# Pair stage of a gated scan and Hadamard FFN kernel: outer products put together by accumulating DMAs

## The chip, the cores and the metric

The kernel runs on one core of one Trainium2 chip. The metric is the device time of one execution in microseconds (us); of several runs the median counts. A profiled execution is a single run with the hardware profiler on. Its engines are named PE (TensorE, matmuls), PEld (its weight loads), DVE (VectorE), ACT (ScalarE), POOL (GpSimd) and SP (SyncE, which here only issues DMAs). A DMA can be issued from SP's queue or from POOL's; the instructions of one engine start in the order of its queue.

## The reference

One transformer layer in float32, with batch 4, sequence 512, model width 512 and hidden width 2048. A gated linear scan takes the place of attention, and the feed-forward part has a Walsh-Hadamard transform ahead of its down projection. The first 490 us of the kernel do everything up to the feed-forward part of batches 2 and 3; what follows concerns that part alone.

```python
def _L0_ffn_ref(x, W1, W2, W3):
    up_gate = jnp.einsum('bsd,hd->bsh', x, W1)
    up_lin = jnp.einsum('bsd,hd->bsh', x, W3)
    hidden = jax.nn.silu(up_gate) * up_lin
    hidden = fwht(hidden)
    out = jnp.einsum('bsh,dh->bsd', hidden, W2)
    return out
...
x = x + _layernorm(_L0_attn_ref(_layernorm(x, axis=-1), ...), axis=-1)
x = x + _layernorm(_L0_ffn_ref(_layernorm(x, axis=-1), ...), axis=-1)
```

The transform `fwht` is folded into `W2` once, early in the kernel, so the down projection reads a transformed `W2`.

## The kernel before

**Seven products.** Every matrix product is cut into 2x2 blocks and made of seven block products instead of eight (Strassen-Winograd). Of each left factor four blocks A11, A12, A21, A22 are loaded and four sums S1 to S4 are made (`combine_left`: L158, L159, L162, L163, four instructions on a tile). Of each right factor the blocks are B11 to B22 and the sums T1 to T4 (`combine_right`, L168 to L173). `ORDER` (L33) names the seven products P1, P2, P6, P5, P7, P3, P4 in the order in which they run, with the PSUM bank of each. Bank X is the running sum of P1, P6, P7 and P4; bank Z that of P5 and P3; bank Y holds P2. So P6 can be added into X only when P1's value has been copied out, P7 only after P6's copy, and so on. After each product its bank goes to its quarter (i, j) of the result. "Fresh" products (P1, P6, P5, P4) are the first to write a quarter, the others (P2, P7, P3) are added to it by VectorE.

**The pair stage.** Batches 2 and 3 go through the up projection together: they are the two column blocks of one wide right factor, so there is one more level of seven products around the seven. The stage is the last loop of the program: it calls `load_down_pair(g)` and `ffn_pair(g, ...)` for g = 0 to 3, then runs the parts that are left, then the tail (residual, layer norm and output of batches 2 and 3). Each run g makes two hidden tiles of each of the two batches (`NS = 2`). Its leading loop goes over the seven outer products in the order `OUTER` (P1, P2, P6, P7, P5, P4, P3), called steps 0 to 6; the inner loop goes over the seven inner ones in `ORDER`. One inner product of one outer product is a leaf: two matmul instructions of 128x128 by 128x256, four records in the profile, all at L879. A run has 49 leaves, counted 1 to 49; leaf 43 is the first of outer P3, which comes last. A bank is evicted after every leaf.

**Leaf weights.** `load_leaf_w(n)` (n = 7g + step + 3, so three outer products ahead; n is counted within a run in what follows, so that step 0 of a run asks for n=3) issues four loads `wl` of 128 KB from SP's queue and then `combine_left` on GpSimd: four instructions on the loaded tile. The tiles rotate through five buffers.

**Accumulators.** The seven outer products also add up to four quarters; each quarter is a 1 MB tile in SBUF of 128 x 2048 numbers (both of `w1` and `w3`, two hidden tiles, 512 columns). Before, there are four of them, `q0` to `q3`. Outer P1 goes into q0 and is copied by ScalarE where fresh (L889), otherwise added by VectorE (L892). Outer P2 goes into q1, with q0 as the base that is added to its fresh products. P6 is added into q0. P7 goes into q3, fresh products by ScalarE. P5 goes into q2 with q0 as the base, and beside it GpSimd adds q3 into q0 (L894) and q2 into q3 (L896), quarter by quarter, eight adds per run. P4 is added into q0, P3 into q2. So in five of the seven outer products all seven evictions are VectorE's.

**What the quarters become.** `hidden(k, h, j)` takes a finished quarter: a SiLU on ScalarE over its first half (L852, 128 x 1024) and two multiplications on VectorE (L860), which write half of a hidden tile `ht` each. When both halves are there, `combine_left` runs on the `ht` tile on GpSimd. Each run thus makes four `ht` tiles: two of batch 2 and two of batch 3. `hidden` is called for q1 and q0 after outer P4, for q3 and q2 at the end of a run.

**What runs between the leaves.** The down projection of the run before (`ffn_out(b, g, True)`) is cut into 28 parts for each batch, one matmul instruction each. In `ffn_pair` they stand in `down` and are spread over leaves `start = 3` to 48: 56 of them in runs g1 to g3 (batch 2's 28, then batch 3's 28), and in g0 those of batch 1. The last 56 follow after g3. Parts read the `ht` tiles and their sums (S1, S2, ...), and every fourth part ends with an eviction (L492 on VectorE, L494 on ScalarE). In g0 the output stage of batch 1 lies beside them (`sums`, `acts`): statistics, `inverse_root` (whose power, L263, is on GpSimd), layer norm, residual, and the output DMAs, which GpSimd issues (L724).

**Right factor.** `combine_pair_late()` is called once ahead of g0: eleven subtractions on VectorE, which make the T sums of the outer level and those of the inner level for the later outer products. `reload_x` brings back the inputs of batch 1.

**What sets the order.** PE and SP run in the order in which the program is written (`tc.manual_schedule` for these two engines). The order on VectorE, ScalarE and GpSimd is chosen when the kernel is built, by a scheduler that looks at data dependences, at `tc.high_priority(offset=...)` and at `tc.issue_after(...)`, which holds an instruction behind another. Evictions have the highest offset (`URGENT`).

Of the kernel before, what the change touches and what calls it, by code (L numbers as in the profile page):

```python
# [11 lines left out]
F32 = mybir.dt.float32  # L12
AF = mybir.ActivationFunctionType
ALU = mybir.AluOpType
P = 128
# [13 lines left out]
T3 = B12  # L29
# [15 lines left out]
def kernel(  # L45
# [40 lines left out]
    )  # L86

# [161 lines left out]
    def behind(what):  # L249


        return tc.issue_after(read[what].ins)
# [210 lines left out]
    def seven(name, multiply, quarter, done=None, add=False, by_tile=False, parts=False):  # L463
# [9 lines left out]
        def make(what, a, bb, which, first, only=None):  # L473
# [23 lines left out]
            if what in ("P2", "P7", "P3") and not by_tile:  # L497
                while scaled and scaled[0][0] == 0:
                    acts.append(scaled.popleft()[1])
                for entry in scaled:  # L500
                    entry[0] -= 1
                for _ in range(min(pace[what], len(sums))):
                    with tc.issue_after(read[what].ins):
                        sums.popleft()()
# [169 lines left out]
    def ffn_out(b, part, parts=False):  # L674
# [21 lines left out]
        def done(i, j, tile=None):  # L696
# [3 lines left out]
            def store(residual, t):  # L700
# [11 lines left out]
                if len(held) == NT:  # L712
                    with tc.issue_after(norm[0].last.ins):
                        for make in held:
                            make()
                    stores(range(NT))
# [59 lines left out]
    def raw(r):  # L776
        return xq[r][:, 0:4]
# [13 lines left out]
    def combine_pair_late():  # L791

        blocks[2] = pair_tile("xt", "xq_3")
        xq.update({T2: blocks[2][:, 0], T1: blocks[2][:, 1]})
        nc.vector.tensor_sub(raw(T2), raw(B21), raw(T4))
        nc.vector.tensor_sub(raw(T1), raw(B22), raw(T2))
        inner(blocks[1], (1,))
        inner(blocks[2])
        combine_right(xq[T4], nc.vector)
# [33 lines left out]

    def ffn_pair(g, down):

        total, start = len(down), 3
        given = 0
        q = {}
        first_of = {"P1": (0, None), "P7": (3, None), "P2": (1, 0), "P5": (2, 0)}
        to_of = {"P1": 0, "P2": 1, "P6": 0, "P7": 3, "P5": 2, "P4": 0, "P3": 2}  # L840

        def accumulator(k):
            pool, tag, bufs = (work, "d", 2) if k == 0 else (xpool, "x", 3)
            q[k] = pool.tile([P, 2, 2, T], F32, tag=tag, name=f"q{k}_{g}", bufs=bufs)

        def part(k, i, j):
            return q[k][:, :, i, ts(j, H)]

        def hidden(k, h, j):

            d, b = q[k], PAIR[j]
            nc.scalar.activation(d[:, 0], d[:, 0], AF.Silu)  # L852
            for n in range(NS):
                m = NS * g + n
                if (b, m) not in hts:
                    hts[b, m] = work.tile(
                        [P, 7, H], F32, tag="ht", name=f"ht_{b}_{m}", bufs=4
                    )
                t = hts[b, m]
                nc.vector.tensor_mul(  # L860
                    t[:, h : h + 3 : 2],
                    d[:, 0, n].rearrange("p (t f) -> p t f", t=2),
                    d[:, 1, n].rearrange("p (t f) -> p t f", t=2),
                )
            return [hts[b, NS * g + n] for n in range(NS)]

        for step, (outer, _, right, _, _) in enumerate(OUTER):
            load_leaf_w(7 * g + step + AHEAD)
            w, x = leaf_w.pop(7 * g + step), xq[right]
            to, base = to_of[outer], None  # L870
            if outer in first_of:
                to, base = first_of[outer]
                accumulator(to)
            ps = {}
            for s, (what, a, bb, which, first) in enumerate(ORDER):
# [9 lines left out]
                fresh = what in ("P1", "P6", "P5", "P4")  # L885
                y = part(to, i, j)
                with tc.high_priority(offset=URGENT):
                    if fresh and outer in ("P1", "P7"):
                        read["copy"] = nc.scalar.copy(y, ps[which])  # L889
                    else:  # L890
                        z = part(base, i, j) if fresh and base is not None else y
                        last = nc.vector.tensor_add(y, ps[which], z)  # L892
                if outer == "P5" and fresh:
                    nc.gpsimd.tensor_add(part(0, i, j), part(0, i, j), part(3, i, j))  # L894
                if outer == "P5" and what in ("P2", "P7", "P3", "P4"):
                    nc.gpsimd.tensor_add(part(3, i, j), part(3, i, j), part(2, i, j))  # L896
                if acts and s in (0, 2, 4):
                    with behind("copy"):
                        acts.popleft()()
                if sums and what in ("P2", "P7", "P3"):  # L900
                    with tc.issue_after(last.ins):
                        sums.popleft()()
                leaf = 7 * step + s + 1
# [4 lines left out]
            if outer == "P4":  # L908
                hidden(1, 0, 0)
                for t in hidden(0, 1, 0):  # L910
                    combine_left(t, nc.gpsimd)
        hidden(3, 1, 1)
        for t in hidden(2, 0, 1):
            combine_left(t, nc.gpsimd)
# [166 lines left out]
    with tc.issue_after(load_x(0).ins):  # L1081

        nc.scalar.activation(unused_t, half_t, AF.Silu)
# [201 lines left out]
    with tc.high_priority(offset=SOON):  # L1285
        combine_pair_late()
# [3 lines left out]
    for g in range(NU // NS):  # L1290
        load_down_pair(g)
        ffn_pair(g, deque(down))
# [41 lines left out]
```

## Time and profile before

| | us |
|---|---|
| runs | 792.66, 791.98, 791.95; median 791.98 |
| profiled execution | 792.25, of which the span of the profile is 790.5 |
| granted TensorE clock | 0.996 of full speed on average |
| runs g0 to g3 begin (first matmul of leaf 1) | 490.23, 553.95, 621.94, 689.44 |
| leaf 49 of each begins | 553.08, 621.08, 688.58, 755.25 |
| last 56 parts | 756.1 to 780.5 |
| tail, after the last matmul | 780.5 to 790.5 |

Evictions and combinations of the pair stage, by their rows:

| line, engine, operation | how many | mean of one, us |
|---|---|---|
| L889 ACT copy, a bank to an accumulator | 32 | 0.585 |
| L892 DVE add, a bank and an accumulator | 164 | 0.69 |
| L852 ACT SiLU, half an accumulator | 16 | 1.06 |
| L860 DVE multiplication into `ht` | 32 | 0.71 |
| L894, L896 POOL adds of accumulators | 16 + 16 | 1.27 |
| L158, L159, L162, L163 POOL, on a leaf weight tile | 26 to 28 each | 0.75 to 0.81 |
| the same on an `ht` tile | 16 each | 0.73 to 0.85 |
| L263 POOL power | 6 | 0.87 |

How to read it: the times of the table are counted from the start of the profiled execution. A leaf without a part beside it takes 0.86 from its first matmul to the next leaf's; with the parts a run takes about 67. Rows of a busy engine say nothing of the end unless another engine waits for it, so what matters is which engine TensorE waits for, and where.

### The profile page before, as it was taken

The page shows a single profiled execution, that of the slowest core. Times are in us where ns is not written, and L with a number is a line of the kernel's source. Part 1 is how long each engine was busy: PE and PEld are TensorE (multiplying, and loading weights), DVE is VectorE, ACT ScalarE, POOL GpSimd, SP SyncE. Part 2 cuts the span into 40 slices and gives each one's busy share as a digit, 9 for nine tenths or more (in the row PEclk, how much of TensorE's full clock was granted, in tenths as well). Part 3 has the DMA queues.
Part 4 walks back from the last instruction along what each step waited for, and adds up shares of the span by engine and source line. Part 5 has one row for each costly group of instructions (what it writes and reads, how often), then busy time and mean ns, then how long its engine had stood idle before and what let it go on. Part 6 is the DMA issues. An engine that isn't in the chain of part 4 may idle for free.

```text
span 790.5 us, 10222 instructions
## 1 busy us (share of the span) xinstructions
PE 776.3 (98%) x3608; PEld 670.1 (85%) x3608; DVE 564.2 (71%) x1093; ACT 246.9 (31%) x348; POOL 245.5 (31%) x319
## 2 busy tenths in 40 slices
PE   9999999999999999999999999999999999999994
PEld 7888788888888888888888888888788888888884
DVE  6789889799789774477455459868755655765676
ACT  4374754543436212344223412011321200111112
POOL 2111202112213110001001005088947646672452
PEclk9999999999999999999999999999999999999998
DMA  9997445776997982538246736341521412141012
GB/s 296 398 340 299 156 198 180 218 258 244 339 336 289 340 325 102 160 150 347 94 187 200 267 78 221 131 122 33 195 80 54 157 53 58 49 166 54 1 53 108
DMA packets 78148, 144.93 MB, mean 183 GB/s; under 512 B 6160, under 2 KB 55952, under 8 KB 77712
## 3 DMA queue, kind: packets, MB, share of 16 engines
q1 hardware_dynamic: 68032, 96.82, 38.1%
q0 software_dynamic: 9344, 46.14, 14.9%
q10 hardware_dynamic: 720, 1.31, 0.4%
q8 instruction: 29, 0.48, 0.2%
q14 instruction: 23, 0.19, 0.1%
HBM read 97.06 MB, written 47.19 MB: 182 GB/s over the span
## 4 chain that ended last, share of the span: by engine, by line
PE 88%; DVE 5%; DMA 2%; POOL 1%; issue 1%; SPq 0%; ACT 0%; POOLq 0%; DVEq 0%
PE X_f L517 13%; PE X_po L684 13%; PE X_u L879 11%; PE X_a L517 10%; PE Z_po L684 7%; PE Z_f L517 6%; PE Z_u L879 5%; PE Z_a L517 5%; PE X_y L624 3%; PE Y_f L517 3%; PE Y_po L684 3%; PE Y_a L517 3%; PE Y_u L879 3%; PE Z_y L624 2%; DMA w2p<-in_W_dram 1%
## 5 line engine op out<-in xcount | busy, mean ns | idle before, releaser
L684 PE MATMUL X_po<-w,ht 128*128 128x256 f32 x512 | 132.1, 379 | 0.1
L517 PE MATMUL X_f<-xt_f,w 128*128 128x256 f32 x512 | 121.2, 380 | 0.1
L879 PE MATMUL X_u<-xq,wl 128*128 128x256 f32 x448 | 114.4, 381 | 2.3 <-ACT q L889 0.8
L517 PEld LDWEIGHTS X_f<-xt_f,w 128*128 128x128 f32 x512 | 96.8, 190 | 14.5 <-DVE d_f L492 0.5
L684 PEld LDWEIGHTS X_po<-w,ht 128*128 128x128 f32 x512 | 97.2, 190 | 13.7 <-DVE f L492 0.5
L879 PEld LDWEIGHTS X_u<-xq,wl 128*128 128x128 f32 x448 | 84.2, 190 | 17.1 <-issue 3.6
L892 DVE TENSOR_TENSOR q<-X_u,q 128x512 f32<-128x512 f32 x88 | 60.8, 691 | 42.6 <-PE X_u L879 41.7
L494 ACT COPY d_f<-X_f 128x512 f32<-128x512 f32 x48 | 28.0, 584 | 131.8 <-PE X_f L517 115.7
L684 PE MATMUL Z_po<-w,ht 128*128 128x256 f32 x256 | 66.4, 379 | 0.0
L492 DVE TENSOR_TENSOR f<-X_po,f 128x512 f32<-128x512 f32 x51 | 34.9, 685 | 36.9 <-PE X_po L684 36.9
L517 PE MATMUL Z_f<-xt_f,w 128*128 128x256 f32 x256 | 60.5, 379 | 0.0
L879 PE MATMUL Z_u<-xq,wl 128*128 128x256 f32 x224 | 57.6, 379 | 0.0
L684 PEld LDWEIGHTS Z_po<-w,ht 128*128 128x128 f32 x256 | 48.6, 190 | 6.8 <-DVE f L492 0.2
L517 PEld LDWEIGHTS Z_f<-xt_f,w 128*128 128x128 f32 x256 | 48.6, 190 | 6.6
L263 POOL TENSOR_TENSOR rs_f<-rs_f,power 128x2 f32<-128x2 f32 x16 | 13.4, 840 | 117.8 <-DVE nm_f L364 73.5
L852 ACT ACTIVATE q<-q 128x1024 f32<-128x1024 f32 x16 | 16.9, 1057 | 103.8 <-DVE q L892 58.2
L879 PEld LDWEIGHTS Z_u<-xq,wl 128*128 128x128 f32 x224 | 42.5, 190 | 6.0 <-DVE q L892 0.3
L892 DVE TENSOR_TENSOR q<-Z_u,q 128x512 f32<-128x512 f32 x48 | 33.1, 689 | 20.1 <-PE Z_u L879 19.5
L158 POOL TENSOR_TENSOR wl<-wl 128x256 f32<-128x256 f32 x28 | 21.3, 762 | 77.4 <-DMA wl<-s_w 70.2
L494 ACT COPY d_a<-X_a 128x512 f32<-128x512 f32 x36 | 21.1, 585 | 67.8 <-PE X_a L517 67.6
L889 ACT COPY q<-X_u 128x512 f32<-128x512 f32 x24 | 14.0, 584 | 89.4 <-PE X_u L879 76.8
L179 POOL DMA_DIRECT2D s_w<-w x24 | 13.1, 547 | 72.5 <-DVE w L163 56.9
(205 smaller groups left out, 1459.2 us busy)
## 6 DMA issues: line engine op xcount, KB each, us to landing
w<-s_w SPq DMA_DIRECT2D x32, 896.0 KB, 6.4
s_w<-w POOLq DMA_DIRECT2D x24, 896.0 KB, 6.9
wl<-s_w SPq DMA_DIRECT2D x112, 128.0 KB, 2.7
w<-in_W_dram SPq DMA_DIRECT2D x32, 256.0 KB, 6.4
wi<-s_wi SPq DMA_DIRECT2D x6, 896.0 KB, 9.3
wf<-s_wf SPq DMA_DIRECT2D x6, 896.0 KB, 5.4
wg<-s_wg SPq DMA_DIRECT2D x6, 896.0 KB, 6.3
w_h<-w2p POOLq DMA_DIRECT2D x8, 512.0 KB, 5.7
```

The costliest lines, as they stand in the source:

```text
L158: eng.tensor_add(t[:, S1], t[:, A21], t[:, A22])
L179: nc.gpsimd.dma_start(out=saved[key], in_=t)
L263: read["power"] = nc.gpsimd.tensor_tensor(r, r, power_t[:, 0:n], ALU.pow)
L492: read[what] = nc.vector.tensor_add(to, ps[which], to)
L494: read["copy"] = nc.scalar.copy(to, ps[which])
L517: nc.tensor.matmul(ps[:, n, :], w[:, a, c, :], xt[:, bb, c, :], start=first and n == 0 and c == 0, stop=c == 1, skip_group_check=True,)
L624: nc.tensor.matmul(ps[:, t, :], og[:, a, c, ts(t, P)], w[c][:, bb, :], start=first and t == 0 and c == 0, stop=c == 1, skip_group_check=True,)
L684: nc.tensor.matmul(ps[:, t, :], hts[b, m][:, a, ts(t, P)], w[m][:, W2[bb], :], start=first and k == 0, stop=m == ms[-1], skip_group_check= ...
L852: nc.scalar.activation(d[:, 0], d[:, 0], AF.Silu)
L879: nc.tensor.matmul(ps[which][:, k, :], w[:, k, a, :], x[:, bb, :], start=first and k == 0, stop=True, skip_group_check=True,)
L889: read["copy"] = nc.scalar.copy(y, ps[which])
L892: last = nc.vector.tensor_add(y, ps[which], z)
```

## The change

It concerns `ffn_pair` and what lies beside it in the pair stage.

- Five accumulators A to E instead of four. Each outer product has one of its own (`ROLE`): P1 in A, P2 in B, P6 in C, P7 in D, P5 in E, and then P4 in A and P3 in C again. They are allocated once, and from run to run the roles rotate: A takes what was B, B what was D, D what was A.
- The fresh products of every outer product but P3 are copied by ScalarE; all else is added by VectorE. There is no base any more, and GpSimd's adds are gone.
- The outer products are put together by DMAs that add (`accum_op=ALU.add`) one whole accumulator of 1 MB to another, from SBUF to SBUF, issued by GpSimd (`gather`). They are issued after the last leaf of an outer product: B += A after P2, C += A after P6, D += C after P7, C += E after P5, and E += D and A += D after P4. P3 is added to what C holds then.
- The SiLUs and multiplications are placed by hand after certain leaves (`after_leaf`): B's after leaf 37, 39 and 40 of its run, C's, A's and E's after leaves 2 to 13 of the next run (written 51 to 62, from which 49 is taken). In the last run B's multiplications and all of C, A and E are placed among the last 28 parts and behind them.
- In g1 to g3 the parts begin after leaf 10 instead of leaf 3. In g3 only half of the 56 parts are spread over the leaves; the other 28 run right after leaf 49.
- `combine_pair_late` gives a list of eleven instructions, one after each of leaves 1 to 11 of g0.
- Within `ffn_pair` all engines run in the written order (`tc.manual_schedule()` without a list of engines), and the holds `issue_after` do nothing there (`after`).

```diff
+    acc, after_leaf = {}, {}
+    ROLE = {"P1": "A", "P2": "B", "P6": "C", "P7": "D", "P5": "E", "P4": "A", "P3": "C"}
+    GATHER = {
+        "P2": (("B", "A"),), "P6": (("C", "A"),), "P7": (("D", "C"),),
+        "P5": (("C", "E"),), "P4": (("E", "D"), ("A", "D")),
+    }
+
+    def hidden(d, g, b, h, combine):
+
+        def gate():
+            read["copy"] = nc.scalar.activation(d[:, 0], d[:, 0], AF.Silu)
+
+        def product(n):
...
+            nc.vector.tensor_mul(
+                t[:, h : h + 3 : 2],
+                d[:, 0, n].rearrange("p (t f) -> p t f", t=2),
+                d[:, 1, n].rearrange("p (t f) -> p t f", t=2),
+            )
+            if combine:
+                combine_left(t, nc.gpsimd)
+
+        return [gate] + [partial(product, n) for n in range(NS)]
+
     def ffn_pair(g, down):
 
-        total, start = len(down), 3
+        last = g == NU // NS - 1
+        total, start = len(down), 10 if g else 3
...
+        if not acc:
+            for k in "ABCDE":
+                pool, tag, bufs = (work, "d", 2) if k in "AC" else (xpool, "x", 3)
+                acc[k] = pool.tile([P, 2, 2, T], F32, tag=tag, name=f"acc_{k}", bufs=bufs)
+        else:
+            acc.update({"A": acc["B"], "B": acc["D"], "D": acc["A"]})
+        q = dict(acc)
+
+        def gather(to, part):
+            nc.gpsimd.dma_start(
+                out=q[to].rearrange("p n i t -> p (n i t)"),
+                in_=q[part].rearrange("p n i t -> p (n i t)"),
+                accum_op=ALU.add,
+            )
...
+        place(hidden(q["B"], g, PAIR[0], 0, False), (37, 50, 50) if last else (37, 39, 40))
+        place(hidden(q["C"], g, PAIR[1], 0, False), (51, 53, 54))
+        place(hidden(q["A"], g, PAIR[0], 1, True), (55, 57, 58))
+        place(hidden(q["E"], g, PAIR[1], 1, True), (59, 61, 62))
+        if last:
+            total -= 28
 
         for step, (outer, _, right, _, _) in enumerate(OUTER):
             load_leaf_w(7 * g + step + AHEAD)
...
-                fresh = what in ("P1", "P6", "P5", "P4")
-                y = part(to, i, j)
-                with tc.high_priority(offset=URGENT):
-                    if fresh and outer in ("P1", "P7"):
-                        read["copy"] = nc.scalar.copy(y, ps[which])
-                    else:
-                        z = part(base, i, j) if fresh and base is not None else y
-                        last = nc.vector.tensor_add(y, ps[which], z)
-                if outer == "P5" and fresh:
-                    nc.gpsimd.tensor_add(part(0, i, j), part(0, i, j), part(3, i, j))
-                if outer == "P5" and what in ("P2", "P7", "P3", "P4"):
-                    nc.gpsimd.tensor_add(part(3, i, j), part(3, i, j), part(2, i, j))
+                y = q[ROLE[outer]][:, :, i, ts(j, H)]
+                if what in ("P1", "P6", "P5", "P4") and outer != "P3":
+                    nc.scalar.copy(y, ps[which])
+                else:
+                    nc.vector.tensor_add(y, ps[which], y)
+                leaf = 7 * step + s + 1
+                for make in after_leaf.pop(leaf, ()):
+                    make()
...
-            if outer == "P4":
-                hidden(1, 0, 0)
-                for t in hidden(0, 1, 0):
-                    combine_left(t, nc.gpsimd)
-        hidden(3, 1, 1)
-        for t in hidden(2, 0, 1):
-            combine_left(t, nc.gpsimd)
+            for pair in GATHER.get(outer, ()):
+                gather(*pair)
...
+        if not last:
+            after_leaf.update({k - 49: after_leaf.pop(k) for k in sorted(after_leaf)})
+            return
+        b0, b1, gate_c, *c, gate_a, a0, a1, gate_e, e0, e1 = pending
+        steps = {2: b0, 4: b1, 6: gate_c, 9: gate_a, 12: a0, 14: a1, 18: gate_e}
+        for k in range(len(down)):
+            down.popleft()()
+            if k in steps:
+                steps[k]()
+        for make in (*c, e0, e1):
+            make()
...
+    for leaf, make in enumerate(combine_pair_late()):
+        after_leaf.setdefault(leaf + 1, []).append(make)
...
     for g in range(NU // NS):
         load_down_pair(g)
-        ffn_pair(g, deque(down))
+        with tc.manual_schedule():
+            in_order.append(g)
+            ffn_pair(g, deque(down))
+            in_order.clear()
```

## The prediction

> Times are in us from the start of the profiled execution unless they are durations. A leaf is the two matmuls of one inner product; g0 to g3 are the four runs of `ffn_pair`, with leaves 1 to 49 each; n counts the leaf weight tiles of a run, n=3 being the one asked for at its first step. T0 is the end of a run's leaf 49.
>
> **What bounds the kernel now.** I read the busy times first, then the pair stage cut into its four runs, what TensorE waited for there, the timeline around the largest gap, and the DMA rows.
>
> ```profile
> PE 776.3 (98%) x3608; PEld 670.1 (85%) x3608; DVE 564.2 (71%) x1093; ACT 246.9 (31%) x348; POOL 245.5 (31%) x319
> ```
>
> ```profile
> core 0: us, PE busy (x) PEld busy (x) DVE busy (x) ACT busy (x) POOL busy (x), PEclk, DMA share, GB/s
> 490.00:554.00 64.00, 63.10 (x287) 53.54 (x286) 50.59 (x82) 8.24 (x12) 41.09 (x48) 1.00 0.29 91
> 554.00:622.00 68.00, 67.32 (x310) 58.20 (x309) 42.74 (x69) 15.63 (x24) 47.50 (x60) 1.00 0.30 94
> 622.00:689.40 67.40, 66.61 (x309) 58.36 (x308) 41.02 (x63) 8.80 (x12) 41.95 (x52) 1.00 0.26 83
> 689.40:756.10 66.70, 66.70 (x309) 58.45 (x309) 41.62 (x64) 8.81 (x12) 33.11 (x40) 1.00 0.22 75
> 756.10:780.50 24.40, 24.35 (x113) 21.09 (x111) 20.18 (x46) 3.73 (x5) 9.60 (x14) 1.00 0.24 87
> ```
>
> TensorE is the bound, at full clock, and the change leaves its 3608 matmul records as many as they are. In the chain of waits eight records take 1.73, 0.216 each, so 309 records need 66.7: g3 (689.40 to 756.10) has no gap at all, g2 has 0.7, g1 about 1.1, g0 (64.0 for 286) about 2.2. Counted from start to start of neighbouring matmuls in the timeline, the whole stage loses 5.2. More than that cannot be won; vector and scalar work are off the path except where a gap shows them on it:
>
> ```profile
> PEld X_u L879 <- issue: 3.6, 7, 1.2
> PEld X_u L879 <- DVE q L892: 1.4, 2, 0.9
> ```
>
> ```profile
> 622.94 1.06 ACT L852 ACTIVATE q<-q 128x1024 f32<-128x1024 f32 x1 [1.08 <-DVE q L892]
> 623.45 0.38 PE L879 MATMUL Y_u<-xq,wl 128*128 128x256 f32 x1
> ...
> 623.90 0.57 ACT L889 COPY q<-X_u 128x512 f32<-128x512 f32 x1
> ...
> 624.62 0.45 PE L879 MATMUL X_u<-xq,wl 128*128 128x256 f32 x1 [0.79 <-ACT q L889]
> ```
>
> This is the kind of gap: bank X carries a running sum, so P6 may not be added before P1 has been copied out. Here a SiLU stands ahead of the copy, which starts at 623.90. An eviction that is one leaf (0.86) late stops TensorE.
>
> **The work moved.** Fresh evictions go from VectorE to ScalarE: 24 copies per run instead of 8, so 64 x 0.69 = 44 leave VectorE (0.69 is L892's mean) and 64 x 0.585 = 37 arrive on ScalarE (L889's row). POOL loses 32 adds of 1.27, 41 in all. None of this is on TensorE's path; it counts only through the gaps. What comes in are six accumulating DMAs of 1 MB per run, 24 in all, from POOL's queue, and a written order in which one late instruction holds all behind it.
>
> **The price of one gather** is not in this trace. Nearest rows:
>
> ```profile
> q0 software_dynamic: 9344, 46.14, 14.9%
> ...
> wl<-s_w SPq DMA_DIRECT2D x112, 128.0 KB, 2.7
> ...
> xr<-s_x SPq DMA_DIRECT2D x3, 1024.0 KB, 4.9
> ...
> s_wf<-wf POOLq DMA_DIRECT2D x2, 896.0 KB, 9.9
> ```
>
> POOL's queue needs 0.149 x 790.5 / 46.14 = 2.55 of all 16 engines per MB, so 2.7 for one pass over 1.05 MB. A small leaf load (128 KB) lands 2.0 after its issue at best; 0.13 MB at 2.55 is 0.3 of that, so 1.7 goes without data. Low end: 4.9, the plain 1024 KB load (one pass). High end: 9.9 x 8/7 = 11.3, the slowest row of this queue. I take 1.7 + 2 x 2.7 = 7.1: an add has to fetch two operands, so two passes; it lies nearer to 4.9 than to 11.3, as DMA engines are 22 to 30% busy here and that slow row comes from the crowded start. [...]
>
> **Where the gathers stand.** A product is 7 leaves. From leaf 10 on a run has about 1.5 per leaf (g1, g2), 1.2 in g0 and 1.18 in g3, where only 28 parts of the down projection are spread in; so the room is 8.2 to 10.5. Four gathers form a chain: B+=A and C+=A, then D+=C (reads C), then C+=E (writes C), which must land before P3's first add into C at leaf 43. And POOL's queue is in order: B+=A stands behind the combinations of leaf weights n=3 and n=4, in g1 to g3 behind 16 combinations of `ht` too (leaves 57, 58, 61, 62).
>
> (a) Start of g0. VectorE does `ht_7`'s five operations (1.2 + 4 x 0.4 = 2.8) ahead of product 1's P7 add, so leaf 7 comes about 1.4 later than 499.36; the copies now on ScalarE take away the gaps at 504.10 (0.34), 508.60 (0.6) and 517.28 (0.47), all behind VectorE adds. Net 0; the bounds are -1.4 (the delay hidden) and +1.4 (nothing won back).
>
> (b) g0's P3. In the timeline POOL starts n=3 at 514.10, when its load lands, and n=5 at 520.66. B+=A thus starts at 520.7, C+=A 3.4 later; both land at 520.7 + 1.7 + 4 x 2.7 = 533.2, D+=C at 540.3, C+=E at 547.4, and about 1.5 later for two leaf loads of 0.5 MB beside them: 548.9. Leaf 43 starts at 545.41, its add must be done by leaf 45's start, 548.00, so C must be there by 547.2. Stall +1.7, say +2.
>
> (c) g0 to g1. Before lost 1.9 here (550.42, 555.79, 558.40, 568.61, 570.47). After: statistics of the old batch stand in written order among P3's adds, +0.5. E+=D and A+=D wait for C+=E: both land at 549 + 0.6 + 1.7 + 10.8 + 2.5 (`w2` and leaf loads beside them, half of 2.3 MB at 2.55) = 564.6. ScalarE has A's SiLU after leaf 55, ahead of the copies of leaves 56 and 57; with leaves of 0.86 it must start by T0 + 5.5, about 561.6. +3.0. POOL then takes n=3, landed 7.9 after T0 in before and 2 later now, two output DMAs, one root, n=4, and only then `ht`: 9.9 + 2.9 + 1.2 + 0.9 + 2.9 + 4.7 = T0 + 22.5 to the second S2, needed at T0 + 18.5 + 3.5. +0.5. Net 4.0 - 1.9 = +2.1.
>
> (d) g1 to g2: the 1.0 at 624.62 goes (its SiLU now stands between copies); S2 of the second `ht` comes at T0 + 8.7 + 2.9 + 2.9 + 4.7 = 19.2 against 18.5, +0.8. Net -0.2. g2 to g3: -0.2 (691.29). In g1 and g2 the chain has 33 leaves less the first ten at 0.86, about 58 from T0, and ends near T0 + 52: covered.
>
> (e) Leaves 1 to 10 of g1 to g3 have no down parts beside them: a VectorE eviction takes 0.2 + 0.69 against a leaf of 0.86. 0.1 per run, +0.3.
>
> (f) g3's P3. POOL is free for B+=A at T0 + 7.9 + 2 x 2.9 + 4 x 3.1 = 26. The pair lands at 38.5, D+=C at 45.6, C+=E at 52.7. Leaf 43 ends at 8.6 + 33 x 0.86 + 24 x 0.43 = 47.5, one leaf of grace: 48.5. +4.2.
>
> Sum: 0 + 2 + 2.1 - 0.4 + 0.3 + 4.2 = +8.2 on the span of 790.5 (792.25 with what lies around it); the median of the runs is 791.98, so 800.2. `combine_pair_late`, spread over leaves 1 to 11, keeps its eleven operations (in (a)); the last 56 parts and the tail after 780.5 (10.0) are not changed.
>
> **Rivals.** *Faster (788.5).* The gathers take 5 or less: (b) and (f) vanish; POOL finds its `ht` in time, the start wins back 1.3, and (c) to (e) win 2.2 of 3.1. For it: g3 shows the stage can run without a gap. Against: POOL's order in (c). 25%.
> *No change (792.5).* Gathers at 4.9, but (c) keeps 0.5 + 2.0 - 1.9 = +0.6, (d) -0.4, (e) +0.3: +0.5. 15%.
> *Far slower (832).* Three passes, 9.8 each: by the steps of (b) and (f) C+=E is 11 late in g0 and 15 in g3, 4.5 in g1 and g2 each, and A 5 late once: +40. For it: 9.9 for 896 KB. Against: the DMA share of 0.3. 13%.
> *The gathers do not run in the places named*, because POOL's wait for one lets the next leaf weights come late: n=8 is asked for a product ahead, 8 to 10; this needs gathers over 9 and is in the last case.
>
> **Numbers.** My case, +3 to +15: 47%, predicted 800.2. A measurement tells about 0.2% (1.6) from no change: faster 25%, same 15%, slower 60%. Low end 788.5, the faster rival's; the high end 815 takes in gathers of about 8 and leaves out the far slower case.
>
> **What would show it.** Gathers landing 6 to 8 after issue; VectorE's first add into C in P3 waiting for a DMA in g0 and g3, longest there; TensorE gaps at leaves 45 of those runs; in g1's start ScalarE's SiLU of A waiting for a DMA. Gathers under 5.5, or B+=A issued a product earlier than I have it, would make the prediction wrong on the high side; stalls in g1 and g2 as long as in g3, on the low side.

## The result, and the profile after

The changed kernel takes 812.69 us (median of four runs, 812.57 to 813.57) against 792.12 before: a ratio of 1.0261, 95% interval 1.0243 to 1.0279, 20.6 us slower. The profiled execution took 813.57, its span is 811.8. Predicted were 800.2, so the side was right and the size was not.

The head of the page and two rows on DMAs, after:

```profile
span 811.8 us, 10255 instructions
...
PE 784.5 (97%) x3608; PEld 674.3 (83%) x3608; DVE 520.8 (64%) x1029; ACT 283.3 (35%) x412; POOL 226.3 (28%) x311
...
q0 software_dynamic: 12800, 71.31, 30.6%
```

The work moved as announced: VectorE has 43 us less, ScalarE 36 more, GpSimd 19 less (41 of adds, less what it spends on issuing 24 gathers), and the matmul records are as many as before. GpSimd's queue (q0) carries 25.2 MB more. New is that TensorE is busy for 8 us longer with the same records. The stretches in which it lost time show why (columns: stretch, its length, then busy time of each engine; behind them the granted clock, the DMA engines' share and GB/s):

```profile
core 0: us, PE busy (x) PEld busy (x) DVE busy (x) ACT busy (x) POOL busy (x), PEclk, DMA share, GB/s
...
540.00:562.00 22.00, 16.44 (x64) 13.74 (x63) 11.05 (x23) 3.09 (x5) 8.96 (x12) 0.84 0.82 168
562.00:584.00 22.00, 19.12 (x77) 14.88 (x76) 12.01 (x22) 9.95 (x15) 11.90 (x15) 0.92 0.70 221
...
703.00:752.60 49.60, 49.60 (x227) 42.18 (x225) 20.57 (x31) 17.76 (x28) 27.19 (x36) 1.00 0.56 146
752.60:766.00 13.40, 7.79 (x25) 6.21 (x24) 4.40 (x7) 0.00 (x0) 1.75 (x2) 0.75 0.87 176
```

g3 runs without a gap worth naming to 752.6. In the next 13.4 us TensorE gets through 25 records, which need 5.4; it waits for 5.8 (5.6 by the list below, which counts idle time alone) and then runs at a lower clock. What it waited for, by the list of waits (total, times, longest):

```profile
PE X_u L916 <- DVE acc_C L926: 11.2, 2, 5.6
PE X_u L916 <- DVE acc_D L926: 2.7, 1, 2.7
PE X_po L689 <- POOL ht L164: 1.7, 1, 1.7
PE X_u L916 <- DVE acc_A L926: 1.1, 1, 1.1
```

The first row is P3's first add into C, once in g0 and once in g3. The chain of gathers that it waits for starts late on GpSimd, in g0 behind leaf weights whose loads keep GpSimd waiting to 516.06, in g3 (from 703.00 on) behind leaf weights and sixteen instructions on `ht`. GpSimd's timeline, the first gather of g0 and of g3:

```profile
516.06 0.72 POOL L163 TENSOR_TENSOR wl<-wl 128x256 f32<-128x256 f32 x1 [20.09 <-DMA wl<-s_w]
...
521.76 0.91 POOL L891 DMA_DIRECT2D acc_B<-acc_A  x1
...
728.49 0.73 POOL L168 TENSOR_TENSOR ht<-ht 128x256 f32<-128x256 f32 x1
729.16 0.85 POOL L891 DMA_DIRECT2D acc_B<-acc_A  x1
```

The chain of waits shows what was late behind it, and behind the second row (start, length, what):

```profile
535.85 8.91 DMA acc_D<-acc_C
...
545.32 6.95 DMA acc_C<-acc_E
552.36 0.70 DVE acc_C L926
...
553.19 2.04 PE X_u L916 x4
...
564.34 7.35 DMA wl<-s_w
...
575.89 0.74 POOL rs_f L268
...
577.78 0.69 DVE acc_D L926
578.51 1.48 PE X_u L916 x4
```

C += E lands at 552.26 and leaf 45 of g0 starts at 553.19. The four records from there stretch over 2.04; four records without a wait show as 1.03. In g1 a leaf weight load takes 7.35, GpSimd waits for it, the root of batch 1's norm stands behind it in GpSimd's queue, the residual behind the root on VectorE, and the add into D behind the residual.

Counted as in the prediction, from start to start of neighbouring matmuls beyond 0.216, the pair stage loses this:

| place | forecast change | before | after | of it slow records |
|---|---|---|---|---|
| start of g0 | 0 | 2.1 | 1.5 | |
| P3 of g0, leaf 45 | +2 | 0 | 8.5 | 2.8 |
| start of g1 | +2.1 | 1.9 | 5.8 | 1.7 |
| starts of g2 and g3 | -0.1 | 1.2 | 3.7 | |
| P3 of g3, leaf 45 | +4.2 | 0 | 8.3 | 2.5 |
| sum | +8.2 | 5.2 | 27.8 | 7.0 |

That is 22.6 more. The span grew by 21.3, since 1.3 less lies between the last matmul's start and the end (9.1, 10.4 before). The last output DMA lands at 787.36 in the span of 790.5 before and at 809.98 of 811.8 after, and what fills the rest the profile does not show.

### The profile page after: what moved, and what is told of

It is laid out like the page before. It is cut to its first block, busy times and chain, and to the rows that moved or that the text cites. A ratio compares the mean times of both kernels' runs of the same rounds, so it can differ in the third digit from the quotient of the medians.

```text
span 811.8 us, 10255 instructions
## 1 busy us (share of the span) xinstructions
PE 784.5 (97%) x3608; PEld 674.3 (83%) x3608; DVE 520.8 (64%) x1029; ACT 283.3 (35%) x412; POOL 226.3 (28%) x311
## 4 chain that ended last, share of the span: by engine, by line
PE 83%; DMA 6%; DVE 4%; POOL 3%; issue 2%; SPq 1%; POOLq 0%; DVEq 0%; ACT 0%
PE X_f L522 13%; PE X_po L689 12%; PE X_a L522 10%; PE X_u L916 8%; PE Z_f L522 6%; PE Z_po L689 6%; PE Z_a L522 5%; PE Z_u L916 4%; PE X_y L629 3%; PE Y_f L522 3%; DMA wl<-s_w 3%; PE Y_po L689 3%; PE Y_a L522 3%; DMA acc_C<-acc_E 2%; PE Y_u L916 2%
## 5 line engine op out<-in xcount | busy, mean ns | idle before, releaser
L916 PE MATMUL X_u<-xq,wl 128*128 128x256 f32 x448 | 118.4, 393 | 14.9 <-DVE acc_C L926 11.2
L916 PEld LDWEIGHTS X_u<-xq,wl 128*128 128x128 f32 x448 | 86.1, 196 | 32.3 <-issue 14.8
L916 PE MATMUL Z_u<-xq,wl 128*128 128x256 f32 x224 | 59.5, 389 | 0.2 <-ACT acc_D L924 0.2
L163 POOL TENSOR_TENSOR wl<-wl 128x256 f32<-128x256 f32 x28 | 27.4, 977 | 96.5 <-DMA wl<-s_w 96.5
L926 DVE TENSOR_TENSOR acc_C<-X_u,acc_C 128x512 f32<-128x512 f32 x20 | 13.8, 690 | 41.3 <-PE X_u L916 23.3
L522 PE MATMUL X_a<-xt_a,wi 128*128 128x256 f32 x128 | 33.2, 381 | 0.1
L689 PE MATMUL Y_po<-w,ht 128*128 128x256 f32 x128 | 33.1, 384 | 0.0
L522 PE MATMUL X_a<-xt_a,wf 128*128 128x256 f32 x128 | 32.8, 379 | 0.0
```

What stands on the lines that cost most here:

```text
L163: eng.tensor_add(t[:, S1], t[:, A21], t[:, A22])
L522: nc.tensor.matmul(ps[:, n, :], w[:, a, c, :], xt[:, bb, c, :], start=first and n == 0 and c == 0, stop=c == 1, skip_group_check=True,)
L689: nc.tensor.matmul(ps[:, t, :], hts[b, m][:, a, ts(t, P)], w[m][:, W2[bb], :], start=first and k == 0, stop=m == ms[-1], skip_group_check= ...
L916: nc.tensor.matmul(ps[which][:, k, :], w[:, k, a, :], x[:, bb, :], start=first and k == 0, stop=True, skip_group_check=True,)
L926: nc.vector.tensor_add(y, ps[which], y)
```

## The experiments

The theory: the time goes to the gathers' chain, which begins late behind GpSimd's other work and ends after P3 needs C, to loads that queue behind gathers, and to TensorE's clock after each wait. The rivals: the written order itself; a gather that is too slow for the room of a product in any order.

### Without the gathers

```diff
-            for pair in GATHER.get(outer, ()):
-                gather(*pair)
```

> The changed kernel without its 24 accumulating DMAs; the outer products are not put together (the output leaves those sums out). Everything else, the written order, the evictions on ScalarE, the late placing of the SiLUs, stays. Theory G (the gathers: adds into C wait for their chain, and leaf loads queue behind them): TensorE's losses in the pair stage fall from 27.8 us to about 4 (start of g0 1.5, leaves without parts about 2), so 787 to 791. Rival W (the written order as such holds the engines up, the gathers are beside the path): 802 or more. Rival R (a root on GpSimd ahead of a residual in g1, without any DMA): the stall at leaf 14 of g1 stays, 2.8 us.

Measured: 794.71 us, ratio to before 1.0042 (1.0022 to 1.0062). TensorE loses 7.1 instead of 27.8, and the waits left are these:

```profile
PE X_po L689 <- POOL ht L164: 1.3, 1, 1.3
PE X_u L916 <- DVE acc_A L926: 1.0, 1, 1.0
PE X_u L916 <- DVE acc_D L926: 0.7, 1, 0.7
```

So 18 of the 20.6 hang on the gathers. The time is still 4 us above the theory's range: the start of g1 loses 3.7 without any gather, because GpSimd still waits there for leaf weights that come behind `w2`, with the root (wait for D, 0.7) and the hidden tiles' sums (wait for `ht`, 1.3) behind it.

### The clock and the gathers by themselves

> Not the computation: bursts of 28 and 20 matmuls of the kernel's shape (128x128 by 128x256), with a wait of TensorE between them of 1 to 17 us, each length three times; then 1 MB accumulating DMAs from SBUF to SBUF, plain copies of the same size, pairs of gathers, leaf-sized loads, and loads issued behind a gather, with nothing beside them. Theory C (a long wait costs twice, since TensorE's records take 0.427 instead of 0.216 for some us after it): none after waits below 2, always after waits above 7, in between by chance; the extra cost is 1.5 to 3 us a time whatever the length of the wait. Rival: records are slow only where gathers run beside them, and here they stay at 0.216. Gathers: 6.9 to 7.0 alone, the second of a pair 5.4 to 6 later; plain copy 4 to 5; loads issued 1 us behind a gather land after it, 7 to 8 after their issue instead of 2.0 to 2.2.

This kernel does not compute the layer; it has 30 waits of TensorE. Afterwards:

| wait, us | waits | with slow records after | extra time by them, us |
|---|---|---|---|
| 1.3 to 1.9 | 6 | 0 | |
| 2.3 to 3.2 | 9 | 2 | 1.7, 1.8 |
| 3.7 to 8.3 | 15 | 15 | 1.5 to 3.1, mean 2.2 |

The granted clock shows it around a wait of 1.85 (first row), 3.70 and 8.31:

```profile
129.00:134.00 5.00, 3.31 (x16) 2.63 (x15) 0.85 (x2) 0.58 (x1) 0.00 (x0) 1.00 0.00 0
...
420.00:428.00 8.00, 4.46 (x14) 3.34 (x13) 2.56 (x6) 0.58 (x1) 0.00 (x0) 0.74 0.00 0
...
767.00:778.00 11.00, 2.85 (x7) 2.19 (x7) 8.90 (x18) 0.58 (x1) 0.00 (x0) 0.73 0.00 0
```

No DMA runs beside them (share 0.00 in all three rows), so it is not the gathers' traffic. How the granted clock falls is to be read in the changed kernel: after its waits of 5.6, 2.7 and 5.6 in g0, g1 and g3 it is at half for 6.83, 3.41 and 6.83, beginning at 551.86, 579.16 and 756.65, and it falls to half once more at 807.85, in the tail. These four starts are 27.31, 177.49 and 51.20 apart, which is 8, 52 and 15 times 3.413; if the falls keep to such a grid, waits of the same length can differ. A length that parts the waits with slow records from those without was not found: two waits of 2.3 and 2.8 were followed by slow records, the seven others of 2.3 to 3.2 were not, and one of 3.9 in the kernel of two gathers further down was not.

The DMAs: a gather alone lands 6.93 to 7.10 after its issue (four times), a plain copy of the same 1 MB 4.69 to 4.87, the second of two gathers issued together 5.0 after the first (11.8 after its issue). Four loads of 128 KB land 2.2 to 3.1 after theirs; issued 0.5 or more behind a gather they all land after it (22 loads), the first of them 8.2 to 8.6 after its issue; two loads that came 0.12 behind a gather landed after 2.5. The prediction's 7.1 for a gather, two passes at 2.7 and 1.7 without data, was right. The two passes were an estimate, and the rows of queue q0 fit it: its time rose by 130.6 of all 16 engines (0.306 x 811.8 less 0.149 x 790.5) for 25.2 MB more, 5.2 per MB, against 2.55 per MB in the kernel before. The second gather of a pair, which took 5.0 for its 1.05 MB, comes to 13 GB/s for each of 16 engines.

### Matmuls in place of the waits

```diff
+                if 7 * step + s == 44 and g in (0, 3):
+                    idle = bank(f"idle_{g}")
+                    for _ in range(12):
+                        nc.tensor.matmul(
...
```

> The changed kernel with 12 more matmuls (24 records, 5.2 us) ahead of leaf 45 in g0 and in g3, where TensorE waits 5.7 and 5.8 us for the adds into C; their results are not read. Theory C (after a wait of over 3 us TensorE's records take twice as long for some us, 2.8 in g0 and 2.6 in g3): the waits shrink below 1 us, the records after them stay at 0.216, and the kernel with more work is faster by 5 to 5.5: 806.5 to 808.5. Rival (records are slow for another reason, the gathers' traffic in SBUF): no gain, 812 to 814; if the wait had not been one for C: 822.

Measured: 811.42 (810.45 and 812.39), ratio to before 1.0246 (1.0226 to 1.0267). The timeline of TensorE in g3:

```profile
751.68 5.34 PE L918 MATMUL idle<-xq,wl 128*128 128x256 f32 x24
756.86 1.03 PE L923 MATMUL X_u<-xq,wl 128*128 128x256 f32 x4
757.73 1.03 PE L923 MATMUL Z_u<-xq,wl 128*128 128x256 f32 x4
```

No record after the filled wait is slow. From leaf 44 to leaf 49 g3 takes 11.2, against 14.3 in the changed kernel, with 24 records more. The time of the whole kernel misses the forecast: it is 1.3 below the changed kernel's, and the intervals of the two overlap. The expected 5 us showed up at the two places (4.9 by the profiles) and were given back in part at g1's start, which waits longer (4.0 at leaf 14, with 1.7 of slow records). So the clock behind the waits is shown at the two places, a faster kernel is not.

### Leaf weights combined later, `w2` loaded later

```diff
-        combine_left(t.rearrange("p w s f -> p s w f"), nc.gpsimd)
         leaf_w[n] = t
+        return t
...
+            combine_leaf_w(leaf_w[n - 1] if n > AHEAD and n - 1 in leaf_w else None)
+            load_leaf_w(n)
```

> The changed kernel, but the four GpSimd instructions that combine a leaf weight tile are written one outer product later than its loads, behind the gathers of that product. So a gather no longer stands behind a load that has not landed. Theory G, by order of GpSimd's queue: in g0 B+=A is issued near 514 instead of 521.8, C+=E lands before leaf 43, no stall in P3 of g0; in g3 the chain starts 3 to 6 us earlier and the stall of 5.8 shrinks to 0 to 2; g1's stall at leaf 14 goes, since GpSimd does not wait for n=3 ahead of the root: 792 to 799. Rival S (a gather of 7 us is too slow for the room of a product whatever the order): the stalls in P3 stay within 1 us, 808 or more.

Measured: 806.88, 5.8 better than the change, ratio to before 1.0192 (1.0162 to 1.0221). GpSimd's first and fourth gather in g0, by its timeline:

```profile
518.63 0.91 POOL L895 DMA_DIRECT2D acc_B<-acc_A  x1
...
541.91 0.86 POOL L895 DMA_DIRECT2D acc_C<-acc_E  x1 [4.56 <-DMA wl<-s_w]
```

The chain begins 3.1 earlier than in the changed kernel (521.76), still behind n=3, whose last load lands at 515.6, and g0's wait falls from 5.7 to 3.8. In g3 the sixteen instructions on `ht` still stand ahead of B += A (27.4 after leaf 1, 26.2 in the changed kernel), and its wait stays at 5.6. g1's wait at leaf 14 is gone. Neither the theory's time nor the rival's came out: one product of delay was not enough.

```diff
-        load_down_pair(g)
...
+            if step == 3:
+                load_down_pair(g)
```

> The changed kernel, but the 1.8 MB of w2 for a run's down projection are loaded in its fourth outer product instead of at its beginning, where two gathers fill the DMA engines. Theory G, by the DMA engines: the leaf weights n=3 of g1 land some 4.5 us earlier (567 instead of 571.6), so the root, the residual and the add into D come earlier: the loss at leaves 13 to 15 of g1 (5.1 with its slow clock) goes or shrinks below 1, g2's 1.9 as well; P3 of g0 and g3 stays as it is: 804 to 809. Rival S: the start of g1 is set by GpSimd's order alone, 811 to 814.

Measured: 809.14, ratio to before 1.0220 (1.0191 to 1.0250), just above the theory's range. g1's wait at leaf 14 and g2's for `ht` are gone, as the theory had it. P3, which was to stay as it is, did not: in g3 the wait fell to 3.8; in g0 it fell to 3.7, but a second one of 1.7 followed at leaf 47 while the clock was still low, and P3 lost 9.0 there, 8.5 in the changed kernel. And g0 lost 4.4 at leaf 7, with 1.7 of slow records, where the changed kernel loses 1.2. VectorE there, first in the changed kernel:

```profile
497.37 0.41 DVE L164 TENSOR_TENSOR ht<-ht 128x256 f32<-128x256 f32 x1
...
497.71 0.41 DVE L167 TENSOR_TENSOR ht<-ht 128x256 f32<-128x256 f32 x1
```

and with `w2` moved:

```profile
496.47 1.59 POOL L164 TENSOR_TENSOR wl<-wl 128x256 f32<-128x256 f32 x1
...
497.40 0.94 DVE L164 TENSOR_TENSOR ht<-ht 128x256 f32<-128x256 f32 x1
...
498.26 0.94 DVE L167 TENSOR_TENSOR ht<-ht 128x256 f32<-128x256 f32 x1
```

Leaf weights that land early are combined on GpSimd while VectorE works on `ht`, and VectorE's take twice as long (0.94 for 0.41).

### The written order undone

```diff
-        with tc.manual_schedule():
-            in_order.append(g)
-            ffn_pair(g, deque(down))
-            in_order.clear()
+        ffn_pair(g, deque(down))
```

> The changed kernel with the written order undone in ffn_pair alone: VectorE, ScalarE and GpSimd are ordered by the scheduler again, as before the change; gathers, accumulators and placing stay. Theory G (the gathers' chain): the adds into C in P3 still wait for C+=E in g0 and g3, since the chain of four needs some 31 us from the place where GpSimd comes to the first: 803 or more. Rival W (the written order holds the engines up): 795 or less.

Measured: 858.38 (854.42 and 862.34), ratio to before 1.0839 (1.0781 to 1.0897). The rival that blamed the written order is out: without it the kernel is 46 us slower still. TensorE's longest wait, 12.7 in g1, ends with this on ScalarE:

```profile
604.68 1.06 ACT L858 ACTIVATE acc_D<-acc_D 128x1024 f32<-128x1024 f32 x1 [14.19 <-DMA acc_D<-acc_B]
605.65 0.57 ACT L924 COPY acc_C<-Z_u 128x512 f32<-128x512 f32 x1
```

The scheduler put a SiLU that needs a gather ahead of the copies of the leaves, and ScalarE stood for 14 us.

### Six gathers in time

Two edits of GpSimd's order: leaf weights are combined two products after their loads, and batch 3's hidden tiles after leaf 22, behind the first two gathers.

```diff
+            if n - 2 >= AHEAD and n - 2 in leaf_w:
+                place([partial(combine_leaf_w, leaf_w[n - 2])], [7 * step + 2])
             load_leaf_w(n)
...
-        place(hidden(q["E"], g, PAIR[1], 1, True), (59, 61, 62))
+        place(hidden(q["E"], g, PAIR[1], 1, True, not last), (59, 61, 62, 71, 72))
```

> The changed kernel with all six gathers, and GpSimd's written order changed in two places only: a leaf weight tile is combined two outer products after its loads (so behind the gathers), and the eight instructions that combine batch 3's hidden tiles come after leaf 22 of the next run instead of leaf 12, behind B+=A and C+=A. Theory Q (GpSimd's order sets when the chain begins; a gather itself has room in a product): B+=A is issued within 3 us of leaf 14's end in g0 and g3, C+=E lands before leaf 43, both stalls in P3 are below 1 us with no slow records, and g1's root no longer waits for leaf weights: 793 to 798. Rival S (six gathers with the loads beside them are too much for the DMA engines whatever the order): C+=E still lands 2 us or more after leaf 44, 803 or more.

Measured: 793.69 (792.35 to 794.83), ratio to before 1.0020 (1.0010 to 1.0029). GpSimd's gathers in g3, whose leaf 1 starts at 690.45, and TensorE's waits:

```profile
707.94 0.86 POOL L898 DMA_DIRECT2D acc_B<-acc_A  x1
...
713.53 0.88 POOL L898 DMA_DIRECT2D acc_C<-acc_A  x1 [1.79 <-ACT acc_C L934]
...
723.01 0.85 POOL L898 DMA_DIRECT2D acc_D<-acc_C  x1
...
730.72 0.88 POOL L898 DMA_DIRECT2D acc_C<-acc_E  x1 [3.92 <-DMA acc_D<-acc_C]
```

```profile
PE X_u L926 <- DVE acc_A L936: 1.1, 1, 1.1
PE X_u L926 <- ACT acc_D L934: 0.8, 1, 0.8
PE X_u L926 <- DVE acc_C L936: 0.7, 1, 0.7
```

B += A is issued 17.5 after leaf 1 instead of 26.2, C += E lands at 737.68, a fifth of a us after leaf 43's start at 737.48, and g3 waits for C no more; g0 waits 0.9. No record of the pair stage is slow. With the same gathers, accumulators and leaves, 19.0 of the 20.6 us are back. The rival that a gather is too slow for its room is out. The first edit alone (the two lines of `n - 2` above):

> Only the first of the two edits of the kernel with six gathers in time: leaf weights are combined two outer products after their loads; the sixteen instructions on hidden tiles stay ahead of B+=A in g1 to g3. Theory Q: g0's stall in P3 is below 1 us as with both edits; in g3 B+=A is issued near T0 + 21 (leaf weights n=3 and n=4 no longer ahead, 26 before), the chain of four ends near T0 + 48, so the stall there is 0 to 1.5 and no slow records follow: 793 to 797. If the hidden tiles ahead of the gather decide in g3, its stall stays above 3 and costs slow records as well: 799 to 803.

It gave 797.41, ratio 1.0067 (1.0051 to 1.0083): g0's wait for C is 1.3, g3's 2.0 (B += A 23.2 after leaf 1), again without slow records. Waits over 1 in g0 and over 1.5 in g3 were not expected, so the hidden tiles count for some 2 us of that run too.

### Two gathers, and none

Here VectorE adds to a base again, as before the change, and two gathers remain.

```diff
+    BASE = {"P2": "A", "P6": "A", "P7": "C", "P4": "D"}
+    GATHER = {"P5": (("C", "E"),), "P4": (("E", "D"),)}
...
+                    z = q[BASE[outer]][:, :, i, ts(j, H)] if fresh else y
+                    nc.vector.tensor_add(y, ps[which], z)
```

> The changed kernel with two gathers a run instead of six (C+=E after P5, E+=D after P4). The other four are replaced as the kernel before did it: VectorE adds the fresh products of P2 and P6 to A's quarter, P7's to C's, P4's to D's, where ScalarE copied them. Order and places stay. Theory G: C+=E is issued near leaf 36 and lands 7 to 8 us later, before leaf 43, so both stalls in P3 and their slow records (16.8 us together) go; the start of g1 stays as without gathers (4.8 lost), VectorE's seven adds in P2 among the hidden multiplications lose 1 to 2 more: 793 to 798. Rival (VectorE, at seven adds a product in the written order, becomes the bound): 802 or more.

Measured: 799.68 (798.17 and 801.18), ratio 1.0098 (1.0075 to 1.0121). The losses in P3 fall to 0.35, as expected, but g1's start lost 5.3, 3.9 of it at leaf 12, where an add stands behind the residual that waits for GpSimd's root, as at leaf 14 in the changed kernel; the time is 1.7 above the forecast. This wait of 3.9 was not followed by slow records: the granted clock of 554.00 to 622.00 is 1.00.

Then the places of the hidden work, the leaf weights (ten leaves after their loads) and the parts:

```diff
-        total, start = len(down), 10 if g else 3
+        total, start = len(down), 3
...
-        place(hidden(q["C"], g, PAIR[1], 0, False), (51, 53, 54))
-        place(hidden(q["A"], g, PAIR[0], 1, True), (55, 57, 58))
-        place(hidden(q["E"], g, PAIR[1], 1, True), (59, 61, 62))
-        if last:
-            total -= 28
+        place(hidden(q["A"], g, PAIR[0], 1, True), (43, 45, 46))
+        place(hidden(q["E"], g, PAIR[1], 1, False), (50, 55, 57))
+        place(hidden(q["C"], g, PAIR[1], 0, True), (52, 58, 60))
```

> The kernel of two gathers with three more edits: a leaf weight tile is combined on GpSimd ten leaves after its loads are issued; the SiLUs and multiplications of A come right after its last add (leaves 43 to 46), those of E and C after leaves 50 to 60, in the last run among the last parts; the down parts begin after leaf 3 in all runs, and in the last run all 56 are spread again. If the losses named so far are all there are (P3's stalls, the late leaf weights ahead of GpSimd's root in g1, the late S2 in g1 and g2, leaves without parts), 1 to 4 us remain of the 5.2 of the kernel before: 788 to 792, that is within 0.5% of before or below it. If VectorE cannot keep a leaf's pace where adds, multiplications and statistics meet: 794 to 800.

Measured: 800.27, ratio 1.0109 (1.0092 to 1.0126), a miss. The starts of the runs were repaired, and 7.4 were lost at one new place (a wait of 5.2 and slow records): in g3 ScalarE took E's SiLU, which waited 16.7 for a gather, ahead of A's, since the two were written in separate stretches and only the order within a stretch is kept.

On top of it:

```diff
+        place(hidden(q["C"], g, PAIR[1], 0, False), (54, 56, 57))
+        place(hidden(q["E"], g, PAIR[1], 1, True), (58, 60, 62))
...
-    for leaf, make in enumerate(combine_pair_late()):
+    for leaf, make in zip((1, 7, 8, 9, 10, 11, 13, 16, 18, 20, 23), combine_pair_late()):
...
+            if g == NU // NS - 1:
...
+                for k, part in enumerate(down[:20]):
+                    part()
+                    if k % 2 and tail:
+                        tail.pop(0)()
             in_order.clear()
```

> The kernel of two gathers again, with the losses of the run before it taken away one by one: the last SiLUs written in one stretch with the last run (there ScalarE took E's SiLU, which waits for a gather, ahead of A's: 7.5 lost), C's SiLU after leaf 54 and E's after 58, where ScalarE has no copies waiting, the late subtractions of the right factor spread to leaf 23, and two pieces of batch 1's output stage per product in g1 instead of three. What is left by the places known: 0.5 at the start of g0, 0.4 at leaf 41, 0.3 at leaf 46, 0.2 at each start of a run, 0.5 in g1: 2 to 3 us of the 5.2 before: 788.5 to 791, faster than before by 0.1 to 0.4%. If VectorE's seven adds a product leave no room for the rest, the gaps move instead of going: 792 to 796.

Measured: 789.56 (788.97 to 789.95), ratio 0.9966 (0.9954 to 0.9979): faster than before. TensorE's only wait on the list is 0.2, and the stage loses 1.8 of before's 5.2. Last, the same kernel with both gathers done by GpSimd:

```diff
-            nc.gpsimd.dma_start(
-                out=q[to].rearrange("p n i t -> p (n i t)"),
-                in_=q[part].rearrange("p n i t -> p (n i t)"),
-                accum_op=ALU.add,
-            )
+            for k in range(4):
+                y = q[to][:, :, k // 2, ts(k % 2, H)]
+                z = q[part][:, :, k // 2, ts(k % 2, H)]
+                nc.gpsimd.tensor_add(y, y, z)
```

> The fastest kernel so far (two gathers, written order, places tuned), with its two gathers a run done by GpSimd instead, as the kernel before did all of this: four adds of 128x512 for C+=E and four for E+=D, some 10 us of GpSimd a run. If the accumulating DMA is what makes it faster than before: 791 or more, as leaf weights and hidden tiles wait for GpSimd and VectorE's SBUF operations slow down beside it. If the written order and the places make it, and GpSimd has room (28 of 64 us busy): 788.5 to 790.5, the same within 0.15%.

Measured: 788.82 (788.60 to 789.20), ratio to before 0.9962 (0.9949 to 0.9975). The accumulating DMA brings nothing here. What wins the 3.1 us against before is in the rest, which the two kernels share: the written order with its places, the later combining of leaf weights and the fifth accumulator. No run takes these apart.

## Why the prediction was right and wrong

- *The price of a gather* (7.1) was right: 6.93 to 7.10 alone. So were the place where it waits and the cause, GpSimd's queue: B += A issued 520.7 forecast, 521.76 measured in g0; 26 and 26.2 after leaf 1 in g3.
- *Step (b) and step (f), the waits in P3*: the mechanism was right, the size was not. 2 and 4.2 were forecast, 5.7 and 5.8 measured. In g0 the chain ends at 552.3 instead of 548.9: B += A comes 1.1 later, C += A 3.8 after it and lands 9.7 after its issue, D += C takes 8.9 as 0.5 MB of leaf weights go beside it, and from a landing to the next issue some 0.5 go by, twice, for which the sum had nothing. The chain was given 1.5 for loads beside it and needed some 5 for all of this; leaf 43 starts 0.5 earlier besides. In g3 it ends 54.6 after leaf 1 instead of 52.7: 1.1 more for the first pair, 1.1 between landings and issues.
- *The term that was missing*: a wait was counted once, and the clock after it was taken as full without a word. Three of them were followed by slow records, 7.0 together, about half of the 14.4 by which the losses of the pair stage grew more than forecast (22.6 against 8.2). No gap of TensorE in the pair stage before was longer than 1.0, so its profile has no price for this; the experiments with waits alone and with filled waits have. That the granted clock falls when TensorE rests could be read there from the tail alone, where it has 3 records and a clock of 0.78:

```profile
780.00:800.00 20.00, 0.45 (x3) 0.05 (x1) 5.17 (x17) 2.67 (x4) 1.91 (x2) 0.78 0.14 53
```

- *Step (c)*, the start of g1: +2.1 forecast, 4.1 less 1.9 is +2.2 without the slow records. That the two agree is chance, as the cause was another one. Not A's SiLU was late but the root behind leaf weights n=3, which landed at 571.7 behind two gathers and `w2`; the prediction had n=3 at 9.9 after the last leaf of g0 and it came 10.1 after it, but the wait was put on S2 and on A's SiLU and not on the residual ahead of the add into D. A landed at 566.03, 4.4 after g1's first leaf and in time, since P3's longer loss had held that leaf back.
- *Steps (d) and (e)*: -0.1 forecast, +2.4 measured. S2 of the second hidden tile came 1.9 late in g2, where 0.8 was forecast, and the ten leaves without parts lose 0.69 in each of g1 to g3, not 0.1; g3 loses 0.28 more at leaves 12 and 13.
- *Step (a)*: 0 forecast, -0.5 measured.
- *The rivals*: without the gathers the kernel takes 794.7, so the faster rival's 788.5 was not within reach of this order even with a free gather. No change is out at 20.6 us. The third-pass price of the far slower case did not come, and the gathers ran where they were put.

## What to carry to other kernels

A transfer with a product's time of room has that room only if the queue that issues it is free when the product ends: look at what stands ahead of the issue, and whether that waits for a load. Price a long wait of TensorE with 1.5 to 3 us on top, for the clock: here 15 of 15 waits of 3.7 to 8.3 us cost 1.5 to 3.1 in the kernel of waits, of 9 between 2.3 and 3.2 two did, and one of 3.9 in another kernel cost nothing. And before work is moved to DMAs, try the written order with the old operations: here a written order with fitting places and GpSimd's adds took 0.4% off the time, and with DMAs in place of these adds it was no faster.

## What the prediction did not have of the hardware

- In the kernel of 30 waits the 6 under 2 us never slowed the records after them, the 15 of 3.7 or more always did, and the extra time does not grow with the wait: 2.9 after 3.7, 1.9 after 8.3. In the changed kernel the granted clock was at half for 3.41 us after one wait and for 6.83 after two. One wait of 3.9 in another kernel slowed nothing.
- Leaf loads from another queue, issued 0.5 us or more behind a 1 MB gather, landed only after it: the first 8.2 to 8.6 after its issue instead of 2.2.
- Three 128x256 operations of VectorE at g0's start took 0.94 each instead of 0.41 when GpSimd combined tiles beside them (the kernel with `w2` moved).
